# Two attention layers in fp32 on one core: the tensor engine in program order, steps of successive products alternating, eight score chunks in a row

## The chip, the cores and the metric

The kernel runs on one core of a Trainium2 chip. Of the engines of a core four matter here, each with its own queue of instructions: the tensor engine (PE, matrix products into PSUM), the vector engine (DVE), the scalar engine (ACT, activations and copies) and GpSimd (POOL); SyncE (SP) issues nearly all DMAs. The metric is the device time of one execution in microseconds.

## What is computed

Input x is 8 images of 512 channels by 32 x 32 = 1024 tokens, fp32. Two attention layers follow each other, each with a residual.

```python
def layer0(x):                                   # 8 heads of 64 channels
    h = group_norm(x, 32 groups)
    q, k, v = w_qkv @ h + b_qkv                  # 512 channels each
    weight = softmax(q^T k / 8)                  # per head, 1024 x 1024
    a = v @ weight^T
    return x + w_proj @ a + b_proj

def layer1(x):                                   # one head of 512 channels
    h = group_norm(x, 8 groups)
    q, k, v = q_w @ h + q_b, k_w @ h + k_b, v_w @ h + v_b
    attn = softmax(q^T k / sqrt(512))            # 1024 x 1024
    return x + p_w @ (v @ attn^T) + p_b
```

## The kernel before

An image is four chunks of 128 channels (KC = 4), two halves of 512 tokens (HT) or eight chunks of 128 tokens (NS). All matrix products are in fp32. The kernel folds layer 1's weights: w_m (from q_w and k_w) gives its scores as h^T (w_m h), and w_z (from v_w and p_w) gives its values already projected.

Per image b the text runs through these stages; those marked * work for image b + 1, since layer 0's q, k, v are made one image ahead, spilled to DRAM and fetched again:

1. layer 0's attention (`attention0`, L372);
2. v* (`by_token`, L296), the projection p (`by_channel`, L289, with `residual`, L621), q* and k* (`conv`);
3. g = w_m h (`conv`), layer 1's scores (`scores1`, L427, two products, one for each half of the first token axis), z = w_z h (`by_token`), the values (`values1`, L473), during which q, k, v of the next image are fetched (hooks, list `order`).

**The large products.** Each is one Strassen-Winograd product (`wino`, L202 to L239): seven products of half size, p = 1, 2, 6, 5, 7, 4, 3, called steps below. A step has two halves, i = 0 and 1, each of 128 output rows by 512 columns. Three PSUM tiles of two halves each, `psa`, `psb` and `psc`, collect them: steps 1 and 2 in a, steps 6, 7 and 4 in b, steps 5 and 3 in c. Within a step the text issues for each i the matmuls (`mm`) and then what reads that half of the tile: after step 1 ACT copies it to t1 (L223); after step 2 `done` makes a first quarter of the result; after 6 DVE makes u = psb + t1 (`upper`, L214); after 7 w, and a quarter from psc; after 4 and 3 the last two quarters. `done` is a copy, an exp with ACT, a bias with DVE (L327), a sum (L315, L450) or a residual (L624), according to the product. A step's matmuls per half are 2 with 512 columns (or 4 with 256), and 4 with 512 in `values1`; each fp32 matmul stands as two records in the trace. The operands of the seven products are sums of quarters, made on DVE (`left_sums` L140, `right_sums` L154), and put into the list `background`; after each step `run_background(back)` issues two or more entries of it, and `hooks` issues what is given for that step.

**Layer 0's attention.** A block is a pair of heads (hp) with a half of the tokens (tb): eight blocks per image. A score chunk is two matmuls of 64 rows, one for each head (L387), ACT's exp (L394) and DVE's running sum (L396, L398). The order of a block is four score chunks, four value chunks (L407, two matmuls of 64 columns), four score chunks, four value chunks. The row sums of a block (`reciprocals`, L340: matmuls with ones L352, reciprocal L354, minimum L355, POOL's sum L356, a DMA out and two back, L358 to L368, which spread r over partitions) are issued after the first four score chunks of the next block, and the product a = av x r (`scaled`, L420) after its second four. The list `extra` (entries for each half of a block) brings in the group norm and operand sums of the next image.

**Who sets the order.** The text gives the dependencies. Each engine's own order is decided by a scheduler with priorities, in before for PE too: it moves matmuls of neighbouring halves, steps, products and stages among each other. Pools: 33 slots of 4 KB per partition for images, factors and exps (`big`, NBIG), 3 PSUM tiles of two halves (`ps_sc`, for scores and for psa, psb, psc), 2 PSUM tiles of one half (`ps_acc`), 3 weight tiles (`wpool`), 1 slot for each of t, u, w and half (`upool`).

Of the kernel before, what the change touches and what calls it, by code (L numbers as in the profile page):

```python
# [9 lines left out]
F32 = mybir.dt.float32  # L10
# [7 lines left out]
NBIG = 33  # L18
# [10 lines left out]
def two_attention_blocks_kernel(  # L29
# [33 lines left out]

    def pcols(name):
        i = 4 * PARAMS.index(name)
        return par[:, i : i + 4]
# [14 lines left out]
    class GroupNorm:  # L81
# [18 lines left out]
        def group_mean(self, ps):  # L100
            mean, var = self.mv[:, :, 0], self.mv[:, :, 1]
            nc.tensor.matmul(ps, gm[:, self.layer, :], mean, start=True, stop=True)

            self.gmean = small.tile([P, KC], F32, tag="gmean", name=f"gmean_{self.uid}")
            nc.vector.tensor_copy(self.gmean, ps)
            d = small.tile([P, KC], F32, tag="d", name=f"d_{self.uid}")
            nc.vector.tensor_sub(d, mean, self.gmean)
            d2 = small.tile([P, KC], F32, tag="d2", name=f"d2_{self.uid}")
            nc.vector.tensor_mul(d2, d, d)
            self.dv = small.tile([P, KC], F32, tag="dv", name=f"dv_{self.uid}")  # L110
            nc.vector.tensor_add(self.dv, d2, var)

        def affine(self, ps):
            nc.tensor.matmul(ps, gm[:, self.layer, :], self.dv, start=True, stop=True)
# [39 lines left out]
    def right_sums(lo, hi, t124, sub):  # L154
# [4 lines left out]
        steps = []  # L159
        for j in range(n):  # L160
            steps.append(lambda j=j: sub(t1[j], b12[j], b11[j]))
            steps.append(lambda j=j: sub(t2[j], b22[j], t1[j]))  # L162
            steps.append(lambda j=j: sub(b12[j], b22[j], b12[j]))
            steps.append(lambda j=j: sub(t4[j], b21[j], t2[j]))
        return {1: b11, 2: b21, 3: b22, 4: t4, 5: t1, 6: t2, 7: b12}, steps

    def main_path(ctx):
# [34 lines left out]
        def wino(uid, mm, done, order=(1, 2, 6, 5, 7, 4, 3), hooks=(), back=2):  # L202
# [4 lines left out]
            ran = set()  # L207

            def u_tile(what, i):
                return upool.tile([P, HT], F32, tag=f"{what}{i}", name=f"{what}{i}_{uid}")  # L210
# [5 lines left out]
            for p in order:  # L216
                if bank[p] not in ps:
                    ps[bank[p]] = sc_tile(f"ps{bank[p]}_{uid}")
                for i in range(2):
                    mm(p, i, ps[bank[p]][:, i, :], bank[p] not in ran)  # L220
# [14 lines left out]
                ran.add(bank[p])  # L235
                run_background(back)
                if hooks:
                    for f in hooks.pop(0):
                        f()  # L239
# [49 lines left out]
        def by_channel(wf, hf, uid, done, **kw):  # L289
            def mm(p, i, ps, start):  # L290
                for k in range(2):
                    nc.tensor.matmul(ps, wf[p][:, k, ts(i, P)], hf[p][k], start=start and k == 0, stop=k == 1, skip_group_check=True)  # L292
# [3 lines left out]
        def by_token(wf, hf, name, **kw):  # L296
# [4 lines left out]
            def mm(p, i, ps, start):  # L301
                for jj in range(2):
                    for k in range(2):
                        nc.tensor.matmul(  # L304
# [35 lines left out]
        def reciprocals(total, uid, across):  # L340
# [6 lines left out]
            if across:  # L347
                sums = acc_tile(f"sums_{uid}")[:, : 2 * P].rearrange("p (a b) -> p a b", a=2)
            else:
                sums = sc_tile(f"sums_{uid}")[:, 0, : 2 * P].rearrange("p (a b) -> p a b", a=2)  # L350
            for i in range(4):
                nc.tensor.matmul(sums[ts(i, 32), :, :], ones[:, :32], total[:, :, ts(i, P)], start=True, stop=True)  # L352
# [19 lines left out]
        def attention0(b, q, k, v, extra):  # L372
            a = channel_tiles(f"a0_{b}")
            ending = []
            NB = 4
            for hp in range(KC):
                for tb in range(2):
                    uid = f"0_{b}_{hp}_{tb}"
                    total = pair_tile(f"sum_{uid}")
                    av = acc_tile(f"av_{uid}")  # L380
                    prev = None
                    for part in range(NS // NB):
                        es = []
                        for s in range(part * NB, (part + 1) * NB):
                            sc = sc_tile(f"sc_{uid}_{s}")
                            for j in range(2):
                                nc.tensor.matmul(  # L387
                                    sc[:, j, :],
                                    k[hp][j * 64 : (j + 1) * 64, ts(s, P)],
                                    q[hp][j * 64 : (j + 1) * 64, ts(tb, HT)],  # L390
                                    start=True, stop=True,
                                )
                            e = pair_tile(f"e_{uid}_{s}")
                            nc.scalar.activation(e, sc, AF.Exp, scale=(C // 8) ** -0.5)  # L394
                            if s == 1:
                                nc.vector.tensor_add(total, prev, e)  # L396
                            elif s > 1:
                                nc.vector.tensor_add(total, total, e)  # L398
                            prev = e
                            es.append(e)  # L400
                        if ending:
                            ending.pop(0)()
                        for f in extra.pop(0) if extra else ():
                            f()
                        for s in range(part * NB, (part + 1) * NB):
                            for j in range(2):
                                nc.tensor.matmul(  # L407
                                    av[j * 64 : (j + 1) * 64, :],
                                    v[s // 2][:, s % 2, hp * P + j * 64 : hp * P + (j + 1) * 64],
                                    es[s - part * NB][:, j, :],  # L410
                                    start=(s == 0), stop=(s == NS - 1),
                                )

                    r = {}

                    def sums(uid=uid, total=total, r=r):
                        r[0] = reciprocals(total, uid, False)

                    def scaled(hp=hp, tb=tb, av=av, r=r):
                        nc.vector.tensor_mul(a[hp][:, ts(tb, HT)], av, r[0])  # L420

                    ending += [sums, scaled]
            assert not extra
            return a, ending


        def scores1(b, gf, hf, uid):  # L427
# [5 lines left out]
            tiles = {}  # L433
            halves = lambda t: (t[:, :HT], t[:, HT:])
            ef = {p: [] for p in range(1, 8)}
            for j in range(2):

                def mm(p, i, ps, start):
                    for k in range(2):
                        nc.tensor.matmul(  # L440
# [29 lines left out]
                wino(f"sc_{uid}_{j}", mm, done)  # L470
            return e, total, ef

        def values1(b, zf, ef, r, xt, uid, hooks):  # L473
            def mm(p, i, ps, start):
                for k in range(4):
                    nc.tensor.matmul(  # L476
# [15 lines left out]
            wino(f"av_{uid}", mm, done, hooks=hooks)  # L492
# [9 lines left out]
        def natural(wt, nm):  # L502
            ts_ = [pair_tile(f"nat{nm}_{h}") for h in range(2)]
            t = [ts_[o // 2][:, o % 2, :] for o in range(KC)]
            for o in range(KC):
                pt = acc_tile(f"tr_w{nm}_{o}")
                for kc in range(KC):
                    nc.tensor.transpose(pt[:, ts(kc, P)], wt[kc][:, ts(o, P)], ident)
# [6 lines left out]
        def product(lhs, rhs, nm):  # L515
            ts_ = [pair_tile(f"prod{nm}_{h}") for h in range(2)]
            for ic in range(KC):
                ps = acc_tile(f"ps_w{nm}_{ic}")
                for kc in range(KC):
                    nc.tensor.matmul(ps, lhs[kc][:, ts(ic, P)], rhs[kc], start=(kc == 0), stop=(kc == KC - 1))  # L520
# [4 lines left out]
        def bias_product(dst, lhs, vec, add, nm):  # L525
            for oc in range(KC):
                ps = acc_tile(f"ps_b{nm}_{oc}")
                for kc in range(KC):
                    nc.tensor.matmul(
# [7 lines left out]
        def prologue():  # L537
# [7 lines left out]
            for c in range(KC):  # L545
                norm.stats(c, h0[c])
            product(wq, wk, "m")
# [8 lines left out]
            for n in "vqk":  # L556
                background.extend(first[n][1][:2])
                if n == "v":
                    background.extend(steps)
                background.extend(first[n][1][2:])  # L560
            v = by_token(weight_factors(first["v"][0]), hf, "v0_0", back=6)
# [7 lines left out]
            k = conv(weight_factors(first["k"][0]), hf, pcols("bk0"), "k0_0")  # L569
            norm1.group_mean(acc_tile("gmean_0_1")[:, :KC])  # L570
# [13 lines left out]
        for b in range(B):  # L584
# [12 lines left out]
            a, ending = attention0(b, q, k, v, extra)  # L597
# [4 lines left out]
            ends = [[ending[0]], [ending[1], lambda: background.extend(steps)]]  # L602
            spill = None
            if more:
# [6 lines left out]
                vn = by_token(weight("v"), hf0, f"v0_{b + 1}", hooks=ends)  # L611
                load_weight()
                store(2, vn)
# [18 lines left out]
            by_channel(weight("p"), af, f"p_{b}", residual)  # L632
            load_weight()
            run_background(len(background))
# [9 lines left out]
            if more:  # L644
                qn = conv(weight("q"), hf0, pcols("bq0"), f"q0_{b + 1}", hooks=[[mean], [], [affine], [normed]])
                load_weight()
                store(0, qn)
                background.extend(steps1)
                kn = conv(weight("k"), hf0, pcols("bk0"), f"k0_{b + 1}")
                load_weight()  # L650
                store(1, kn)
            else:
                mean()
# [3 lines left out]
            run_background(len(background))  # L657

            g = conv(weight("m"), hf1, ubias, f"g1_{b}")
            load_weight()  # L660
            stiles = [pair_tile(f"sg{i}_{b}") for i in (1, 2, 4)]
            halves = lambda t: (t[:, :HT], t[:, HT:])
            gf, steps = left_sums(
# [3 lines left out]
            background.extend(steps)  # L667
# [14 lines left out]
            z = by_token(weight("z"), hf1, f"z1_{b}", hooks=[[], [], [], [], [sums]], back=3)  # L682
            load_weight()
# [5 lines left out]
            zf, steps = left_sums(  # L689
# [3 lines left out]
            background.extend(steps)  # L693
# [3 lines left out]
            if more:  # L697
# [8 lines left out]
                for n, (i, c) in enumerate(order):  # L706
                    hooks[2 + n // 3].append(lambda i=i, c=c: fetch(i, c))
            values1(b, zf, ef, state["r"], xt, f"1_{b}", hooks)

# [11 lines left out]
        nc.tensor.matmul(ps[0:1, 0:1], both, ones[:, 0:1], start=True, stop=True)  # L721
        nc.vector.tensor_scalar(flag, ps[0:1, 0:1], -1.0, float(P), ALU.mult, ALU.add)

# [179 lines left out]
```

## Time and profile before

| | us |
|---|---|
| median of 3 runs | 3096.59 (3093.09 to 3098.21) |
| the profiled execution | 3092.8 |
| its span | 3090.9 |
| PE busy | 3042.8 (98%) |
| DVE busy | 1857.2 (60%) |
| ACT busy | 759.3 (25%) |
| POOL busy | 146.9 (5%) |
| image period (first score records at 527.0, 901.3, 1275.6, 1650.0) | 374.3 |

In a profile, a group of instructions is named by line, engine, operation and `out<-in`, with `x` for how many there are, then busy time, mean length of one, and the idle time of the engine just before them with what ended most of it. PEld is the load of the stationary operand. A matmul record's length reaches past the start of the next record, since matmuls are pipelined; the distance between starts tells how fast they stream. The largest groups off PE are the exps of layer 0 and the running sums:

```profile
L394 ACT ACTIVATE e<-sc 128x1024 f32<-128x1024 f32 x512 | 483.8, 1030 | 557.8 <-PE sc L387 550.9
L398 DVE TENSOR_TENSOR sum<-sum,e 128x1024 f32<-128x1024 f32 x384 | 466.3, 1214 | 74.7 <-ACT e L394 53.5
L354 DVE RECIPROCAL rc<-sums 128x256 f32<-128x256 f32 x72 | 125.9, 1749 | 14.9 <-issue 14.9
L420 DVE TENSOR_TENSOR a<-av,r 128x512 f32<-128x512 f32 x64 | 44.0, 688 | 33.6 <-DMA r<-rows 33.0
```

### The profile page before, as it was taken

The page shows a single profiled execution, that of the slowest core. Times are in us where ns is not written, and L with a number is a line of the kernel's source. Part 1 is how long each engine was busy: PE and PEld are TensorE (multiplying, and loading weights), DVE is VectorE, ACT ScalarE, POOL GpSimd, SP SyncE. Part 2 cuts the span into 40 slices and gives each one's busy share as a digit, 9 for nine tenths or more (in the row PEclk, how much of TensorE's full clock was granted, in tenths as well). Part 3 has the DMA queues.
Part 4 walks back from the last instruction along what each step waited for, and adds up shares of the span by engine and source line. Part 5 has one row for each costly group of instructions (what it writes and reads, how often), then busy time and mean ns, then how long its engine had stood idle before and what let it go on. Part 6 is the DMA issues. An engine that isn't in the chain of part 4 may idle for free. (4 is left out here: it accounts for less than half of the span.)

```text
span 3090.9 us, 26887 instructions
## 1 busy us (share of the span) xinstructions
PE 3042.8 (98%) x10322; PEld 1374.1 (44%) x10322; DVE 1857.2 (60%) x2445; ACT 759.3 (25%) x925; POOL 146.9 (5%) x119
## 2 busy tenths in 40 slices
PE   7999999999999999999999999999999999999898
PEld 5535444354543545335453354534445354443344
DVE  4376465864658646585366754567546764547754
ACT  1142111521124111351114411143111431105210
POOL 0000000000000000000000100000000000000000
PEclk9999999999999999999999999999999999999999
DMA  6412314023140332302332132411325023040101
GB/s 250 168 71 93 126 52 167 18 89 126 64 158 18 109 126 92 106 20 107 126 125 76 48 125 77 164 41 45 126 88 174 21 73 140 29 140 18 38 0 35
DMA packets 78295, 283.55 MB, mean 92 GB/s; under 512 B 9360, under 2 KB 16336, under 8 KB 71632
## 3 DMA queue, kind: packets, MB, share of 16 engines
q1 hardware_dynamic: 77744, 281.61, 25.8%
q8 instruction: 83, 1.36, 0.2%
q14 instruction: 52, 0.43, 0.0%
q10 hardware_dynamic: 416, 0.16, 0.0%
HBM read 207.51 MB, written 74.22 MB: 91 GB/s over the span
## 5 line engine op out<-in xcount | busy, mean ns | idle before, releaser
L394 ACT ACTIVATE e<-sc 128x1024 f32<-128x1024 f32 x512 | 483.8, 1030 | 557.8 <-PE sc L387 550.9
L398 DVE TENSOR_TENSOR sum<-sum,e 128x1024 f32<-128x1024 f32 x384 | 466.3, 1214 | 74.7 <-ACT e L394 53.5
L387 PE MATMUL sc<-q_again,k_again 64*128 64x512 f32 x1792 | 432.4, 603 | 0.0
L407 PE MATMUL av<-e,v_again 128*64 128x512 f32 x1792 | 409.2, 598 | 0.0
L387 PEld LDWEIGHTS sc<-q_again,k_again 64*128 64x128 f32 x1792 | 168.0, 186 | 260.7 <-issue 214.6
L407 PEld LDWEIGHTS av<-e,v_again 128*64 128x64 f32 x1792 | 118.6, 136 | 259.9 <-issue 224.8
L356 POOL TENSOR_TENSOR all_recs<-all_recs,rc 128x256 f32<-128x256 f32 x72 | 97.8, 1358 | 1604.6 <-DVE rc L354 1604.6
L440 PE MATMUL psa_sc<-g,h 128*128 128x512 f32 x256 | 125.4, 602 | 11.7 <-ACT t_sc L223 5.8
L354 DVE RECIPROCAL rc<-sums 128x256 f32<-128x256 f32 x72 | 125.9, 1749 | 14.9 <-issue 14.9
L396 DVE TENSOR_TENSOR sum<-e,e 128x1024 f32<-128x1024 f32 x64 | 78.3, 1224 | 91.1 <-ACT e L394 91.1
L451 ACT ACTIVATE e<-e 128x512 f32<-128x512 f32 x96 | 60.2, 630 | 261.3 <-DVE e L450 261.3
L476 PE MATMUL psa_av<-e,z 128*128 128x512 f32 x256 | 120.1, 601 | 0.0
L129 ACT ACTIVATE h<-h,b,s 128x1024 f32<-128x1024 f32 x30 | 37.1, 1240 | 192.0 <-DMA h<-in_x 158.9
L440 PEld LDWEIGHTS psa_sc<-g,h 128*128 128x128 f32 x256 | 46.7, 190 | 81.3 <-issue 47.8
L476 PEld LDWEIGHTS psa_av<-e,z 128*128 128x128 f32 x256 | 46.7, 190 | 53.2 <-issue 40.1
L292 PE MATMUL psa_g<-h,w_m 128*128 128x512 f32 x128 | 65.0, 622 | 4.0 <-ACT h L129 3.3
L214 DVE TENSOR_TENSOR u_sc<-psb_sc,t_sc 128x512 f32<-128x512 f32 x32 | 22.1, 691 | 77.0 <-PE psb_sc L440 77.0
L387 PE MATMUL sc<-q,k 64*128 64x512 f32 x256 | 65.3, 616 | 0.0
L214 DVE TENSOR_TENSOR w_sc<-psb_sc,t_sc 128x512 f32<-128x512 f32 x32 | 22.1, 691 | 71.8 <-PE psb_sc L440 71.8
L304 PE MATMUL psa_z<-w_z,h 128*128 128x256 f32 x256 | 64.6, 385 | 0.0
L420 DVE TENSOR_TENSOR a<-av,r 128x512 f32<-128x512 f32 x64 | 44.0, 688 | 33.6 <-DMA r<-rows 33.0
L440 PE MATMUL psc_sc<-sg,h 128*128 128x512 f32 x128 | 63.6, 599 | 0.6
(281 smaller groups left out, 4299.7 us busy)
## 6 DMA issues: line engine op xcount, KB each, us to landing
x<-in_x SPq DMA_DIRECT2D x36, 512.0 KB
h<-in_x SPq DMA_DIRECT2D x32, 512.0 KB
r<-rows SPq DMA_DIRECT2D x128, 128.0 KB
out<-x SPq DMA_DIRECT2D x64, 256.0 KB
w_p<-sums_p SPq DMA_DIRECT2D x8, 1792.0 KB
spill<-v SPq DMA_DIRECT2D x28, 512.0 KB
w_m<-sums_m SPq DMA_DIRECT2D x8, 1792.0 KB
spill<-q SPq DMA_DIRECT2D x28, 512.0 KB
```

What stands on the lines that cost most here:

```text
L292: nc.tensor.matmul(ps, wf[p][:, k, ts(i, P)], hf[p][k], start=start and k == 0, stop=k == 1, skip_group_check=True)
L304: nc.tensor.matmul(ps[:, ts(jj, C // 2)], hf[p][k][:, ts(2 * i + jj, P)], wf[p][:, k, :], start=start and (jj, k) == (0, 0), stop=(jj, k) ...
L354: nc.vector.reciprocal(rc, sums)
L356: nc.gpsimd.tensor_tensor(all_recs, all_recs, rc, ALU.add)
L387: nc.tensor.matmul(sc[:, j, :], k[hp][j * 64 : (j + 1) * 64, ts(s, P)], q[hp][j * 64 : (j + 1) * 64, ts(tb, HT)], start=True, stop=True,)
L394: nc.scalar.activation(e, sc, AF.Exp, scale=(C // 8) ** -0.5)
L396: nc.vector.tensor_add(total, prev, e)
L398: nc.vector.tensor_add(total, total, e)
L407: nc.tensor.matmul(av[j * 64 : (j + 1) * 64, :], v[s // 2][:, s % 2, hp * P + j * 64 : hp * P + (j + 1) * 64], es[s - part * NB][:, j, :], ...
L440: nc.tensor.matmul(ps, hf[p][k][:, ts(2 * j + i, P)], gf[p][k], start=start and k == 0, stop=k == 1, skip_group_check=True)
L451: nc.scalar.activation(dst, dst, AF.Exp, scale=scale)
L476: nc.tensor.matmul(ps, zf[p][k // 2][:, k % 2, ts(i, P)], ef[p][k], start=start and k == 0, stop=k == 3, skip_group_check=True)
```

## The change

- Every matmul and transpose goes through a local function that keeps it in program order on PE: PE now issues them as the text does. The other engines are still ordered by the scheduler.
- `wino` is cut into `step(p)`. A product issues its step 1, then `finish()`, the tail of the product before it (its steps 4 and 3, and the entries of `after`), then the four middle steps, (6, 2, 5, 7) or (2, 5, 6, 7), and leaves its own steps 4 and 3 as the next tail. The t tiles have two slots.
- What stood behind a product in the text (loads of weights, stores of the spill, operand sums of its result) moves into `after`; the hooks of q and values1 are regrouped; `values1` runs 4 background entries per step.
- `attention0` issues eight score chunks, then `scaled` of the block before, then eight value chunks, then its own row sums, in a `ps_acc` tile.
- `right_sums` lists its operations kind by kind; NBIG is 32; the prologue makes v's weight sums earlier.

```diff
+    def matmul(*args, **kw):
+        tc.keep_in_program_order(nc.tensor.matmul(*args, **kw))
...
-NBIG = 33
+NBIG = 32
...
-        def wino(uid, mm, done, order=(1, 2, 6, 5, 7, 4, 3), hooks=(), back=2):
+        tail = []
+
+        def finish():
+            while tail:
+                tail.pop(0)()
+
+        def wino(uid, mm, done, middle=(6, 2, 5, 7), hooks=(), after=(), back=2):
...
-            for p in order:
-                if bank[p] not in ps:
+            def step(p):
+                start = bank[p] not in ps
+                if start:
                     ps[bank[p]] = sc_tile(f"ps{bank[p]}_{uid}")
                 for i in range(2):
-                    mm(p, i, ps[bank[p]][:, i, :], bank[p] not in ran)
+                    mm(p, i, ps[bank[p]][:, i, :], start)
...
+            step(1)
+            finish()
+            for p in middle:
+                step(p)
+            tail.extend([lambda: step(4), lambda: step(3), *after])
...
-            if across:
-                sums = acc_tile(f"sums_{uid}")[:, : 2 * P].rearrange("p (a b) -> p a b", a=2)
-            else:
-                sums = sc_tile(f"sums_{uid}")[:, 0, : 2 * P].rearrange("p (a b) -> p a b", a=2)
+            sums = acc_tile(f"sums_{uid}")[:, : 2 * P].rearrange("p (a b) -> p a b", a=2)
...
+                    for s in range(NS):
+                        sc = sc_tile(f"sc_{uid}_{s}")
+                        for j in range(2):
+                            matmul(
+                                sc[:, j, :], k[hp][ts(j, 64), ts(s, P)], q[hp][ts(j, 64), ts(tb, HT)],
+                                start=True, stop=True,
+                            )
+                        e = pair_tile(f"e_{uid}_{s}")
+                        nc.scalar.activation(e, sc, AF.Exp, scale=(C // 8) ** -0.5)
...
+                    for f in extra.pop(0) if extra else ():
+                        f()
+                    if scaled:
+                        scaled()
                     av = acc_tile(f"av_{uid}")
...
+                    for s in range(NS):
+                        for j in range(2):
+                            matmul(
+                                av[ts(j, 64), :], v[s // 2][:, s % 2, hp * P + j * 64 : hp * P + (j + 1) * 64],
+                                es[s][:, j, :], start=(s == 0), stop=(s == NS - 1),
+                            )
+                    for f in extra.pop(0) if extra else ():
+                        f()
+                    r = reciprocals(total, uid, False)
...
-                vn = by_token(weight("v"), hf0, f"v0_{b + 1}", hooks=ends)
-                load_weight()
-                store(2, vn)
+                vn = by_token(
+                    weight("v"), hf0, f"v0_{b + 1}", hooks=ends, after=[load_weight, lambda: store(2, vn)]
+                )
...
-            wino(f"av_{uid}", mm, done, hooks=hooks)
+            wino(f"av_{uid}", mm, done, middle=(2, 5, 6, 7), hooks=hooks, back=4)
...
-                    hooks[2 + n // 3].append(lambda i=i, c=c: fetch(i, c))
+                    hooks[(2, 4, 5, 6)[n // 3]].append(lambda i=i, c=c: fetch(i, c))
             values1(b, zf, ef, state["r"], xt, f"1_{b}", hooks)
+            finish()
```

## The prediction

> **What bounds the kernel now.** I read the busy shares first, then the costliest groups for idle time with a releaser, then single stretches of the timeline in which the tensor engine (PE) changes its work.
>
> ```profile
> PE 3042.8 (98%) x10322; PEld 1374.1 (44%) x10322; DVE 1857.2 (60%) x2445; ACT 759.3 (25%) x925; POOL 146.9 (5%) x119
> PEclk9999999999999999999999999999999999999999
> L440 PE MATMUL psa_sc<-g,h 128*128 128x512 f32 x256 | 125.4, 602 | 11.7 <-ACT t_sc L223 5.8
> ```
>
> PE is busy for 98% of 3090.9 us, and at full clock in every slice. So a change can win only the remaining breaks, and any new break is paid in full. The last row shows the one kind of break that has a place: PE wants to write psa_sc and is held by ACT, which is still copying from it. This view is of one such place, with the columns start, length, engine and line, and in brackets the idle time before and what ended it:
>
> ```profile
> 400.91 1.98 PE L440 MATMUL psa_sc<-g,h 128*128 128x512 f32 x4 [0.72 <-ACT t_sc L223]
> ...
> 402.93 0.60 ACT L448 ACTIVATE e<-psa_sc 128x512 f32<-128x512 f32 x1 [2.07 <-PE psa_sc L440]
> 403.58 0.30 PEld L440 LDWEIGHTS psa_sc<-g,h 128*128 128x128 f32 x2 [1.51 <-ACT e L448]
> 403.58 1.98 PE L440 MATMUL psa_sc<-g,h 128*128 128x512 f32 x4 [0.69 <-ACT e L448]
> ...
> 405.40 1.88 PE L440 MATMUL psb_sc<-sg,t_h 128*128 128x512 f32 x4
> ...
> 407.12 1.02 PE L440 MATMUL psc_sc<-sg,t_h 128*128 128x512 f32 x2
> 407.39 0.69 DVE L214 TENSOR_TENSOR u_sc<-psb_sc,t_sc 128x512 f32<-128x512 f32 x1 [4.19 <-PE psb_sc L440]
> 408.13 0.30 PEld L440 LDWEIGHTS psb_sc<-sg,t_h 128*128 128x128 f32 x2 [0.82 <-DVE u_sc L214]
> 408.13 1.55 PE L440 MATMUL psb_sc<-sg,t_h 128*128 128x512 f32 x3
> ```
>
> A half step of a score product is four records of 512 columns. Streaming, they start 0.429 us apart (405.40 to 407.12 is four of them). The half from 400.91 should hand over at 402.62; the next half starts at 403.58. In between lies only the exp of the first half (402.93 to 403.53). The two halves are different parts of one tile, psa_sc, but the program's wait is for the tile. **Price of a direct wait behind ACT: 403.58 - 400.91 - 4 x 0.429 = 0.95 us.** At psb_sc the same wait, now behind DVE, is nearly hidden: the half ends its slots at 407.12, DVE reads it until 408.08, and two psc_sc records run meanwhile. Without them PE would stand from 407.12 to 408.13, and the first record after a wait takes 0.53 instead of 0.43: **1.01 + 0.10 = 1.11 us behind DVE.** So before is fast because its scheduler put something else between the halves.
>
> The attention blocks, and two score matmuls that were moved among layer 1's values:
>
> ```profile
> 505.89 1.12 PE L387 MATMUL sc<-q_again,k_again 64*128 64x512 f32 x2
> 506.94 3.70 PE L476 MATMUL psb_av<-e,z 128*128 128x512 f32 x8
> ```
>
> ```profile
> 548.36 3.70 PE L387 MATMUL sc<-q_again,k_again 64*128 64x512 f32 x16
> 551.99 3.65 PE L407 MATMUL av<-e,v_again 128*64 128x512 f32 x16
> 555.58 3.70 PE L387 MATMUL sc<-q_again,k_again 64*128 64x512 f32 x16
> 559.21 0.64 PE L352 MATMUL sums<-sum,ones 128*32 128x256 f32 x8
> ```
>
> Sixteen records of two heads run in pairs, eight slots of 0.429 = 3.43 us; 548.36 to 551.99 is 3.63 and 551.99 to 555.58 is 3.59. Entering the scores costs 0.20, entering the values 0.15.
>
> **The change, part by part.**
>
> *Program order in the large products.* In the built order of the changed kernel each matmul stands where the text issues it. Steps of successive products alternate, but within a step the half i=1 stands directly behind i=0. Every step except 5 has its first half read before the second is written, so it waits; and where two steps on one tile follow each other (6 then 7, or 7 then 4) it waits again. Counting in that order the PE instructions whose wait is on an ACT or DVE read of what the instruction just before it wrote gives 461: 129 behind ACT, 332 behind DVE, over 72 products. In the order of before I can tell 22 such waits; most of the others have one to three matmuls ahead of them. Cost: 129 x 0.95 + 332 x 1.11 = 123 + 369 = **+492**. Bounds: the shortest idle time in these rows (0.69) gives 318; the residual and bias reads take 0.75 instead of 0.69 (L624, L327), which on all 332 gives 512.
>
> *What those stages lose today.* Summed over every record, the time from start to start beyond the cadence is 194 us in the whole kernel, some 80 of it in the stages of large products (the rest: attention's changes of kind, the prologue, the last image's gaps). All of it is replaced: **-80**, bounds 0 and -94 (the latter by pricing each wait of before with the matmuls that stand between).
>
> *Split score pairs.* Before moves 34 single score matmuls of the next image among values1. Each runs alone for its two records (505.89 to 506.94 is 1.05 us), where half a pair is 0.43. Seventeen pairs lose 17 x 0.858 = 14.6, and their changes of kind, 34 x 0.35 = 12. After issues them in pairs: **-27**; if the pairs do not reunite, 0.
>
> *Eight chunks in a row.* One entry into the scores and one into the values less per block: 64 x (0.20 + 0.15) = **-22**. Exps on ACT start 0.917 us apart, chunks 0.858; with three score tiles chunk 7 needs exp 4 done at about 5.87 us of the block and starts at 6.11. Cover 0.24 us; if ACT were 0.1 us slower per exp, each block would lose about 0.2, 13 us in all.
>
> *Row sums at the end of the second product.* The sums (0.57 us, before after the first scores of the next block) now stand right after the eighth value chunk, at 14.1 us of the block, and the eighth running sum must be done: DVE needs 7 adds at 1.33 us after the second exp, about 12 us, if nothing is put in. In the built DVE order three blocks of an image have `scaled` (L420) among the adds, which waits for r; r lands 5.3 us after its reciprocal (562.95 to 568.27), so at 7.2 of the block. The adds then end at 14.55: 0.5 us lost in two blocks, and 2.0 in the one that also holds two factor operations of h. 3.0 per image: **+25**, bounds 0 (DVE catches up) and 64 x 2.0 = 128 if every block did this. What queues behind these sums on PE are the next block's scores, and on ACT its exps.
>
> *DVE's queue in the large products.* A wait behind DVE ends when DVE comes to it. In the built DVE order other work stands ahead of such reads: in the scores the sums of g and the subtractions (0.69 each: +1.55), four bn_stats of the image after next (4 x 0.67 = 2.6) and at z's step 6 1.0; 0.9 each in p and q. The scheduler in before lets PE go elsewhere meanwhile. 7.4 per image: **+60**, bounds 0 and 120 (each delay met twice, at both halves).
>
> *Slots, DMAs.* One big slot less, fetches regrouped over four steps, stores and weight loads issued one tail later. SP's queue carries them in the same order, and the fetched q, k land some 10 us before use (h's applies end at 517.9, paired scores start at 527). I cost them at 0; without that cover, one h apply (1.24 us) per chunk would show, 5 us per image, 40 in all.
>
> *The clock.* Before, the granted clock falls to half only after PE gaps of 3.5 us (at 37 and 2925 us); a gap of 3.0 us at 2919 did not do it, nor did halves in which PE stood for a third. After has one gap near 3.6 us per image (scores behind bn_stats). Half a window each is **+10**, bounds 0 and 24. A rule that speaks against the change: the Trainium skill, "TensorE: Matmul & The Clock Gate", section "A second HAM failure mode: psum-queue depth-cycling", says that small idle times of PE between groups of matmuls make its clock swing between half and full. The trace shows full clock through the waits at 400 to 409; by the rule part of the products would run at half speed, where by the trace none does.
>
> Sum: 3091 + 492 - 80 - 27 - 22 + 25 + 60 + 10 = **3549 us**. The profiled run took 3092.8, the median of the runs shown is 3096.6, so I add 3 and say **3552 us**.
>
> **The rivals.**
> - *DVE's queue becomes the bound of the products.* For it: 461 waits now expose every item of its queue, and DVE is already 60% busy. Against: ahead of most reads nothing stands. With twice the queue delays and reads of 0.75: 3552 + 60 + 20 + 14 (the clock's upper bound) = 3646, and up to 3720 with every block's sums late.
> - *The halves do not wait.* If hardware or program lets i=1 write its own half while i=0 is read, the waits fall away and so do today's breaks: 3552 - 492 - 60 - 10 = **2990**, faster. It decides once a direct wait costs under 104 / 461 = 0.23 us, 104 being what the change saves elsewhere (80 + 27 + 22 - 25). Against it: the rows at 403.58, where PE stood with nothing else to do.
> - *Only the shorter part shows.* If each wait costs what its idle column says (0.69 to 0.82) and DVE's queue nothing: 3552 - (492 - 350) - 60 = 3350.
> - *The clock swings.* If a quarter of the products' matmul work (64 of 56 slots and 8 of 112, at 0.429: 1922 us) runs at half clock: 3552 + 480 = 4030. Against: full clock in all slices of before, with 22 such waits, though never this dense.
>
> **How the numbers follow.** Forecast 0.74; DVE bound 0.1; shorter waits 0.08; clock 0.04; no waits 0.04, of which 0.01 ends within 0.2% (6 us, about what a measurement of this kernel can tell from no change). Faster 0.03, same 0.01, slower 0.96. The range goes from 3430 (each wait 0.2 shorter, 92, and half the queue delays, 30) to 3660 (DVE bound at twice its delays); about 0.2 is left out: the shorter waits, the clock, no waits and the upper end of the second case.
>
> **What would show it.** PE busy near 3000 us of a span near 3550, so 85%; about 460 idle times of PE ended by ACT L223, copies and exps, or by DVE u, w and final reads, 0.7 to 0.85 us each in the idle column; attention blocks of 14.65 us where before had 15.0; sums waiting for DVE's sum in three blocks per image; clock full. I am wrong if PE's large products show no idle time ended by the reads of their own tile, or if the clock line leaves 9.

## The result and the profile after

The changed kernel takes 3540.53 us (median of 4 runs, 3535.74 to 3544.32), against 3095.52 us for the kernel before: 1.1437 times as long, 95% interval 1.1417 to 1.1456. The forecast was 3552, in a range of 3430 to 3660. The profiled execution has a span of 3539.7 us at a mean granted clock of 0.988 (before: 3090.9 at 0.995).

These are lines of the page of the changed kernel. Every matmul now has line 66, since all go through the new function.

```profile
span 3539.7 us, 26844 instructions
...
PE 3090.2 (87%) x10322; PEld 1384.5 (39%) x10322; DVE 1853.0 (52%) x2445; ACT 755.2 (21%) x925; POOL 112.6 (3%) x119
...
PEclk9999999999999999999999999999999999999999
...
PE 51%; issue 17%; DVE 15%; ACT 2%; DMA 2%; POOL 1%; SPq 0%; DVEq 0%; ACTq 0%; POOLq 0%
...
L66 PE MATMUL psc_sc<-sg,h 128*128 128x512 f32 x128 | 72.6, 697 | 35.4 <-DVE e L451 35.4
```

PE has the same 10322 records and the other engines as many instructions as before, but PE is idle for 13% of a longer span, and the chain that ended last now has DVE in it for 15% and "issue" for 17% (before, it could be followed back over 6% of the span only, nearly all PE). The last row had 0.6 us of idle time before.

The timeline of layer 1's values shows where the time went (start, length, engine, line; in brackets the idle time before and what ended it):

```profile
572.86 3.60 PE L66 MATMUL psb_av<-t,sz 128*128 128x512 f32 x8
...
576.50 0.69 DVE L225 TENSOR_TENSOR u_av<-psb_av,t_av 128x512 f32<-128x512 f32 x1 [8.82 <-PE psb_av L66]
...
577.24 3.70 PE L66 MATMUL psb_av<-t,sz 128*128 128x512 f32 x8 [0.78 <-DVE u_av L225]
...
580.98 0.69 DVE L225 TENSOR_TENSOR u_av<-psb_av,t_av 128x512 f32<-128x512 f32 x1 [3.79 <-PE psb_av L66]
...
581.73 3.70 PE L66 MATMUL psb_av<-e,z 128*128 128x512 f32 x8 [0.78 <-DVE u_av L225]
...
585.46 0.69 DVE L225 TENSOR_TENSOR w_av<-psb_av,t_av 128x512 f32<-128x512 f32 x1 [3.79 <-PE psb_av L66]
...
586.21 3.70 PE L66 MATMUL psb_av<-e,z 128*128 128x512 f32 x8 [0.79 <-DVE w_av L225]
```

Eight records take 3.43 us of slots, and the halves follow each other at 4.38 to 4.49 us. Each time DVE reads the half just written for 0.69 us and PE does nothing. This is the forecast's direct wait, once per half.

To see the whole, I add for every PE record the time from the start of one to the start of the next beyond its cadence (0.429 us for 512 columns, 0.2146 for 256, a pair of heads counted once):

| us beyond cadence | before | after |
|---|---|---|
| large products, all | 101.9 | 570.1 |
| of it single breaks over 0.7 us (without the two at the group norm's last step) | 20.8 in 23 | 478.7 in 462 |
| attention: entries into scores and values | 54.3 | 26.4 |
| attention: row sums | 9.2 | 27.9 |
| group norm and prologue | 27.6 | 33.3 |
| slots of the work itself | 2885.9 | 2869.6 |

The sums over the rows without the second, which is part of the first, differ by +468.2 - 27.9 + 18.7 + 5.7 - 16.3 = 448.4; the spans differ by 448.8.

### The profile page after: what moved, and what is told of

Its sections match the earlier page's. It is cut to its first block, busy times and chain, and to the rows that moved or that the text cites. A ratio compares the mean times of both kernels' runs of the same rounds, so it can differ in the third digit from the quotient of the medians.

```text
span 3539.7 us, 26844 instructions
## 1 busy us (share of the span) xinstructions
PE 3090.2 (87%) x10322; PEld 1384.5 (39%) x10322; DVE 1853.0 (52%) x2445; ACT 755.2 (21%) x925; POOL 112.6 (3%) x119
## 4 chain that ended last, share of the span: by engine, by line
PE 51%; issue 17%; DVE 15%; ACT 2%; DMA 2%; POOL 1%; SPq 0%; DVEq 0%; ACTq 0%; POOLq 0%
PE sc L66 7%; PE av L66 6%; PE psb_av L66 5%; PE psb_sc L66 4%; DVE sum L405 4%; PE psa_av L66 3%; PE psc_av L66 3%; PE psa_sc L66 3%; PE psc_sc L66 3%; PE psb_g L66 3%; PE psb_k L66 2%; PE psb_z L66 2%; PE psa_g L66 2%; PE psc_g L66 2%; DMA r<-rows 2%
## 5 line engine op out<-in xcount | busy, mean ns | idle before, releaser
L401 ACT ACTIVATE e<-sc 128x1024 f32<-128x1024 f32 x512 | 476.4, 1054 | 541.6 <-PE sc L66 541.6
L66 PE MATMUL sc<-q_again,k_again 64*128 64x512 f32 x1792 | 399.7, 596 | 0.0
L66 PE MATMUL av<-e,v_again 128*64 128x512 f32 x1792 | 396.9, 596 | 0.0
L66 PEld LDWEIGHTS sc<-q_again,k_again 64*128 64x128 f32 x1792 | 167.3, 186 | 211.5 <-ACT e L401 101.9
L369 POOL TENSOR_TENSOR all_recs<-all_recs,rc 128x256 f32<-128x256 f32 x72 | 63.5, 882 | 1815.9 <-DVE rc L367 1815.9
L66 PE MATMUL psc_sc<-sg,h 128*128 128x512 f32 x128 | 72.6, 697 | 35.4 <-DVE e L451 35.4
L66 PE MATMUL psb_p<-t_a,w_p 128*128 128x512 f32 x128 | 64.9, 630 | 18.5 <-DVE x L631 6.7
L66 PE MATMUL psb_sc<-g,h 128*128 128x512 f32 x128 | 62.7, 612 | 19.4 <-DVE w_sc L225 12.5
L66 PE MATMUL psb_z<-w_z,t_h 128*128 128x256 f32 x256 | 67.4, 410 | 13.1 <-DVE u_z L225 6.8
L66 PE MATMUL psb_sc<-sg,t_h 128*128 128x512 f32 x128 | 65.4, 635 | 13.1 <-DVE u_sc L225 13.1
```

The source lines that it names most:

```text
L66: tc.keep_in_program_order(nc.tensor.matmul(*args, **kw))
L369: nc.gpsimd.tensor_tensor(all_recs, all_recs, rc, ALU.add)
```

## The experiments

Each was timed in turns with the kernel before on the same chip; ratios are to that.

**1. Both halves written before they are read.**

```diff
                 for i in range(2):
                     mm(p, i, ps[bank[p]][:, i, :], start)
+                for i in range(2):
                     if p == 1:
```

> The changed kernel, but in a step the matmuls of both halves are issued first and what reads the tile after them; PE stays in program order, the steps and all else as they are. If the loss is the wait of the second half for the reads of the first (theory), 421 of the 461 direct waits go, at 0.95 us each; left are the places where two steps on one tile follow each other (17 times 6 then 7, some 11 times 7 then 4), each now longer, about 1.7 us, since both halves are read after both are written. 3540 - 461 x 1.05 + 28 x 1.8 = about 3105, between 3070 and 3150. If the loss is strict order as such (weight loads that cannot run ahead, kinds of work that alternate more often) or DVE's queue, less than half of it goes: above 3330. If the clock is what costs, the granted clock rises from 0.988 and at most 30 us go.

Measured: 3062.33 us, ratio 0.9888 (0.9872 to 0.9905), clock 0.992. The same stretch of the timeline, PE alone:

```profile
491.31 7.03 PE L66 MATMUL psb_av<-t,sz 128*128 128x512 f32 x16
499.79 7.13 PE L66 MATMUL psb_av<-e,z 128*128 128x512 f32 x16 [1.45 <-DVE u_av L225]
508.30 7.13 PE L66 MATMUL psb_av<-t,z 128*128 128x512 f32 x16 [1.38 <-DVE w_av L225]
515.27 5.31 PE L66 MATMUL psc_av<-e,sz 128*128 128x512 f32 x12
```

Sixteen records run without a break; breaks stand here only where step 7 follows 6, and 4 follows 7, on psb. None between 0.7 and 1.15 us is left in the products of the whole trace; 88 of their 570 us beyond cadence are left (38.5 of them in the values). So one line of order, with program order, steps and attention untouched, takes back more than the whole loss. Strict order on PE is no burden as such: this is 1.1% faster than the kernel before. A scheduler that orders PE freely in this text, with both halves written first, was not run.

**2. The change without program order, and 3. program order without the change.**

```diff
-        tc.keep_in_program_order(nc.tensor.matmul(*args, **kw))
+        nc.tensor.matmul(*args, **kw)
```

> The changed kernel without program order: PE's order is the scheduler's again, all else as changed. Theory: the scheduler puts other matmuls between the halves (18 direct waits behind DVE and 10 behind ACT in its built order, against 332 and 129), so the products cost what they cost before, and attention keeps its gain of some 20 us: 3050 to 3095. If the new order of steps or the tails cost by themselves, it stays above 3200.

Measured: 3103.77 us, ratio 1.002 (1.001 to 1.003), 9 us above the upper end expected. The waits are gone as the theory says: 34 breaks over 0.7 us are left in the products, 32.4 us in all. But of the gain in attention most is gone too. From the start of each record to the next, scores, values and row sums together take 982.9 us here, 990.0 in the kernel before and 964.2 in the changed kernel. And the products take 13.6 us more than in the kernel before: 15 of the 34 breaks, 0.95 each, are waits behind w in the values, where the kernel before has one.

> The kernel before with program order on PE and nothing else. Its text has the halves one behind the other too, and the steps of one product in a row: 548 direct waits in the built order (180 behind ACT, 368 behind DVE). Theory: 3096 + 180 x 0.95 + 368 x 1.05 - 80 (its own breaks) - 27 (split pairs) + 40 (DVE's queue) = about 3585, between 3520 and 3660: slower than the changed kernel, so that alternating steps helped a little and program order alone makes the loss. If the loss needs the other edits, it stays near 3100.

(The same function as in the changed kernel, around every matmul and transpose of the kernel before.) Measured: 3616.08 us, ratio 1.1679 (1.166 to 1.1699); expected 3585, 3520 to 3660. Two lines of its page:

```profile
span 3613.4 us, 26948 instructions
...
PE 3121.4 (86%) x10322; PEld 1357.8 (38%) x10322; DVE 1877.7 (52%) x2445; ACT 763.4 (21%) x925; POOL 146.9 (4%) x119
```

Program order alone makes the loss: the trace has 548 breaks over 0.7 us in the products, as many as were counted ahead. The loss is larger than in the changed kernel; by the traces 58 of the 74 us between the two lie in the products.

**4. The old attention in the changed kernel, and 5. the new attention in the kernel before.** Only `attention0`, its row sums' tile and its ending are exchanged.

```diff
-            a, scaled = attention0(b, q, k, v, extra)
+            a, ending = attention0(b, q, k, v, extra)
```

> The changed kernel with the attention of before: four score chunks, four value chunks, row sums after the first scores of the next block; the rest as changed. Theory: eight in a row saves 22 and the row sums at the end lose about 20, so the two attentions cost nearly the same here (the 27 us of split pairs come from program order and stay): 3540 within 10. If eight in a row is worth its 22 and the sums at the end cost nothing, it is 3562; if the sums are the larger, below 3530.

Measured: 3535.56 us (3534.01 to 3543.23) beside 3540.53: the same within their spread, as the theory has it. Beyond cadence, its entries cost 48.6 us against 26.4 in the changed kernel, and its row sums 9.3 against 27.9: eight chunks in a row win 22.2 and the row sums at the end give 18.6 back, so the new attention is some 4 us the faster. The products of this run are 8.6 us shorter than the changed kernel's, since fewer stretches of half clock fall into them (see the last section).

> The kernel before with the new attention alone (eight chunks in a row, row sums at the end), PE's order left to the scheduler. The forecast's terms give 3096 - 22 + 25 = 3099. The changed kernel without program order came out at 3104 and had 164 score matmuls that stood alone instead of 68 in before; if the new attention brings these, this run is at 3100 to 3110 with as many of them; if the new order of steps does, it is at 3099 or below with about 70.

Measured: 3094.43 us, ratio 0.9989 (0.9979 to 0.9999), as the second case has it. The count in the expectation was a wrong reading, though: 164 is the number of score records in run 2 (two to a matmul) without a partner that starts within 25 ns, and here there are 168. Most of these do run in twos, with the partner up to 312 ns behind. Layer 1's values, the first scores of a block after them, and last the same place in the kernel before:

```profile
511.10 1.12 PE L380 MATMUL sc<-q_again,k_again 64*128 64x512 f32 x2
512.16 3.70 PE L462 MATMUL psb_av<-e,z 128*128 128x512 f32 x8
...
532.22 6.27 PE L380 MATMUL sc<-q_again,k_again 64*128 64x512 f32 x26
538.42 1.94 PE L398 MATMUL av<-e,v_again 128*64 128x512 f32 x8
```

```profile
527.00 2.84 PE L387 MATMUL sc<-q_again,k_again 64*128 64x512 f32 x10
529.77 3.65 PE L407 MATMUL av<-e,v_again 128*64 128x512 f32 x16
```

The 26 records take 6.20 us to the first value, which is 14 slots of 0.429 and the entry of 0.20, and the 10 in the kernel before take 2.77, 6 slots and the entry. Thirteen and five slots would do if every record shared its slot, so in each case one matmul runs alone, beside the three that stand among the values. Counted so (a partner within 300 ns), 68 records run alone in the kernel before, in run 2 and here. A free scheduler moves the same few score matmuls out under either attention, and each holds PE for two slots instead of sharing them. That loss, priced in the prediction, stays in runs 2 and 5 and goes with program order.

**6. One tile for each half, in one place.**

```diff
+                    if two and p == 5:
+                        ps["c"] = [acc_tile(f"psc{i}_{uid}") for i in range(2)]
```

> The changed kernel, but in layer 1's two score products psc is two tiles of one half each (from the pool of the row sums), so that step 3's second half need not wait for the read of its first. Order and work are as changed; 16 direct waits of 461 go (316 behind DVE instead of 332). Theory: the wait is the program's, by tile, and the chip can write one half while the other is read: 14 of these waits were 2.58 us long in the changed kernel's trace, since DVE had sums or statistics ahead, and two about 1; with the slower first records and the clock drops that follow the long ones 16 x 0.1 and 14 x 0.7 more: 3540 - 38 - 2 - 10 = 3490, between 3480 and 3505. If the chip itself held the write until the read is over, the time would stay at 3540.

Measured: 3497.01 us (3496.45 to 3499.68), 43.5 less than the changed kernel. The changed kernel first, then this one, at step 3 of the first score product:

```profile
481.15 1.88 PE L66 MATMUL psc_sc<-sg,h 128*128 128x512 f32 x4
...
482.20 0.68 DVE L451 TENSOR_TENSOR e<-psb_sc,t_sc 128x512 f32<-128x512 f32 x1
...
483.58 1.23 DVE L458 TENSOR_TENSOR sum<-sum,e 128x1024 f32<-128x1024 f32 x1 [0.69 <-ACT e L452]
484.72 0.68 DVE L451 TENSOR_TENSOR e<-psc_sc,u_sc 128x512 f32<-128x512 f32 x1
...
485.46 1.62 PE L66 MATMUL psc_sc<-sg,h 128*128 128x512 f32 x2 [2.43 <-DVE e L451]
```

```profile
480.05 3.60 PE L66 MATMUL psc_sc<-sg,h 128*128 128x512 f32 x8
...
482.48 1.22 DVE L462 TENSOR_TENSOR sum<-sum,e 128x1024 f32<-128x1024 f32 x1 [0.69 <-ACT e L456]
...
483.48 1.88 PE L66 MATMUL psb_sc<-sg,t_h 128*128 128x512 f32 x4
...
483.62 1.28 DVE L455 TENSOR_TENSOR e<-psc_sc,u_sc 128x512 f32<-128x512 f32 x2
```

In the changed kernel the first half could be read at about 483, but DVE first waits for an exp and adds a running sum for 1.23 us; PE stands for 2.43 us behind it. With two tiles the eight records run through, and DVE reads both halves later. So the wait belongs to the tile. At two of the sixteen places DVE is early enough to read the first half while PE writes the second; this is one:

```profile
3050.95 3.60 PE L66 MATMUL psc_sc<-sg,h 128*128 128x512 f32 x8
...
3052.87 0.69 DVE L455 TENSOR_TENSOR e<-psc_sc,u_sc 128x512 f32<-128x512 f32 x1
```

The second half's four records start at 3052.67 and stream on at 0.43 us while DVE reads, so the chip does not hold the write here. The gain is made up otherwise than the theory has it. The 16 waits, 38.1 us, are gone, but part of what DVE had ahead is met at later waits (the one behind u on psb grows from 0.98 to 1.55 us in the mean), so that all breaks together fall by 26 us; the rest is mainly the half clock that followed the long breaks.

**7. What alternating the steps is worth.** Program order and both halves first, in the kernel before, whose steps of one product stand in a row.

```diff
+        tc.keep_in_program_order(nc.tensor.matmul(*args, **kw))
...
                     mm(p, i, ps[bank[p]][:, i, :], bank[p] not in ran)
+                for i in range(2):
                     if p == 1:
```

> The kernel before with program order on PE and both halves of a step written before they are read; its steps stay 1, 2, 6, 5, 7, 4, 3 of one product in a row, its attention is the old one. What is left are waits where two steps on one tile follow each other: 1 then 2 and 7 then 4, 52 behind ACT and 64 behind DVE stand directly behind each other in the built order. Theory: two reads now end such a wait, about 1.4 us behind ACT and 1.6 behind DVE: 73 + 102 = 175, against some 50 in the changed kernel with both halves first (3062): about 3187, between 3150 and 3230. That would be what alternating the steps is worth. If alternating is worth nothing beyond the halves, it is at 3062.

Measured: 3217.94 us, ratio 1.0394 (1.0378 to 1.041), in the expected range. The trace has 117 breaks over 0.7 us in the products, 172.8 us (116 and 175 were expected), against 38 and 60.4 in run 1. The two runs differ by 156 us, and their spans by 155; 131 of that lie in the products, 17 in the attention with its row sums, the rest in the prologue and the group norm. So alternating steps, with the regrouped operand sums that belong to it, is worth some 130 us once the halves don't wait; with waiting halves (run 3 and the changed kernel) it was worth 58.

**8 to 10. Towards a faster version**, each on top of the one before.

```diff
-            wino(f"av_{uid}", mm, done, middle=(2, 5, 6, 7), hooks=hooks, back=4)
+            wino(f"av_{uid}", mm, done, middle=(2, 6, 5, 7), hooks=hooks, back=4)
```

> The version with both halves written before they are read, and values1's middle steps as 2, 6, 5, 7 instead of 2, 5, 6, 7, so that step 5 lies between the two steps on psb. Theory: the eight waits of 1.61 us at 6 then 7 go: 3062 - 13 = 3049. If step 6's operand (a sum on DVE, issued after step 2) is late, up to 1.5 us come back per image: 3061.

Measured: 3048.49 us, ratio 0.9836 (0.982 to 0.9853). As expected: the eight breaks are gone from the trace, since step 5 now covers the reads of step 6.

```diff
-                    if scaled:
-                        scaled()
                     av = acc_tile(f"av_{uid}")
...
+                    if scaled:
+                        scaled()
                     r = reciprocals(total, uid, False)
```

> As the one before, and in attention the product a = av x r of the last block is issued after the value chunks, behind the running sums. Theory: the row sums' waits for DVE (0.3 to 1.6 us in three blocks per image, 15 us above 0.5 and 23 in all) shrink: 3049 - 15 = 3034. If the scheduler puts the product where it was, or the value tile is then freed too late for the next row sums, no change or slower.

Measured: 3049.36 us, ratio 0.9841 (0.9825 to 0.9858): no change. DVE's order is the scheduler's, and the product stayed among the running sums.

```diff
-                            nc.vector.tensor_add(total, total, e)
+                            tc.keep_in_program_order(nc.vector.tensor_add(total, total, e))
...
-                        nc.vector.tensor_mul(a[hp][:, ts(tb, HT)], av, r)
+                        tc.keep_in_program_order(nc.vector.tensor_mul(a[hp][:, ts(tb, HT)], av, r))
...
+                    for _ in range(2):
+                        for f in extra.pop(0) if extra else ():
+                            f()
                     r = reciprocals(total, uid, False)
...
-                    extra[8 + i].append(f)
+                    extra[8 + i].append(lambda f=f: tc.keep_in_program_order(f()))
```

> The version with both halves first and 2, 6, 5, 7 in values1 (3048), and in attention DVE in program order for the running sums, the product a = av x r and the operand sums of h, all of the latter two behind the running sums of their block. Theory: the row sums' waits go (23 us of 27 in the trace of that version), and a later reciprocal costs nothing, since the first running sum has 0.8 us to spare: 3048 - 20 = 3028. If the running sums themselves are late behind the reciprocal and the operand sums, the waits of one or two blocks per image stay: 3040. If it is above 3048, holding DVE's order costs more than it saves.

Measured: 3030.55 us (3028.32 to 3031.22), ratio 0.9782 (0.9769 to 0.9796), near the 3028 expected. First a block of the changed kernel whose row sums wait:

```profile
675.57 5.32 PE L66 MATMUL av<-e,v_again 128*64 128x512 f32 x24
...
679.91 1.29 DVE L166 TENSOR_TENSOR t_h<-h 128x512 f32<-128x512 f32 x2
681.12 1.22 DVE L405 TENSOR_TENSOR sum<-sum,e 128x1024 f32<-128x1024 f32 x1
...
682.39 0.64 PE L66 MATMUL sums<-sum,ones 128*32 128x256 f32 x8 [1.50 <-DVE sum L405]
```

and then a block of this version:

```profile
568.23 7.88 DVE L406 TENSOR_TENSOR sum<-sum,e 128x1024 f32<-128x1024 f32 x6
...
570.76 7.09 PE L66 MATMUL av<-e,v_again 128*64 128x512 f32 x32
...
576.02 0.68 DVE L423 TENSOR_TENSOR a<-av,r 128x512 f32<-128x512 f32 x1
...
577.78 0.64 PE L66 MATMUL sums<-sum,ones 128*32 128x256 f32 x8
...
578.35 7.14 PE L66 MATMUL sc<-q_again,k_again 64*128 64x512 f32 x32
```

In the first, two operand sums of h stand ahead of the last running sum and PE waits 1.50 us for it. In the second, six running sums go in a row, the product behind them is over at 576.70, and PE goes from values to row sums to scores without idle time. No block's row sums wait for DVE any more. This version is 2.2% faster than the kernel before, with all of its work.

## Why the prediction was right

The mechanism is the one forecast, and the sum came out 12 us above the time. That it is so near has some luck in it: DVE's queue was put 23 us too high and the clock some 15 too low. By its own terms, with what the trace after shows (beyond cadence):

- **Direct waits, +492 for 461.** 462 breaks over 0.7 us are there. 421 of them lie between 0.7 and 1.15 and sum to 402.3, 0.96 each; with the slow first record behind a wait, some 0.1, that is within the priced 0.95 to 1.11, and all 462 at that price are some 490. Runs 1 and 6 remove them by the text's order and by the tile, and the time follows; run 3 makes them without the rest of the change. This cause is shown.
- **Before's own losses, -80.** The products lost 101.9, of which 7.1 are two breaks at the last image's and the prologue's group norm, and those stay. In the changed kernel less than 20 of the products' 570.1 are neither a break over 0.7, nor a slow first record, nor half clock, so over 80 were replaced.
- **DVE's queue, +60.** Too large. Over a plain 0.96 the 41 breaks above 1.15 us hold 37 us (and the items listed add to 7.0 per image, not 7.4). The place was right in part: 14 of them, of 2.6 us, are at psc of the scores. In the second product they stand behind the statistics of a later image, as forecast, but in the first behind a running sum, which the forecast did not name; z's step 6 shows no delay (1.01), its step 3 does (1.34).
- **Split pairs -27 and entries -22.** The slots of the work fell by 16.3, the entries by 27.9: 44 of 49. Run 4 gives the entries of eight chunks in a row alone as 22.2.
- **Row sums, +25.** 18.7, in the three blocks per image that were named.
- **Clock, +10.** Too small, and its reading of the kernel before was wrong. There the clock fell at 37.4, before PE's break began (37.8 to 41.1), and at 2925.1, 0.9 us into the second of two breaks, so neither fall shows that a break of 3.5 us is needed. In the changed kernel eleven stretches of half clock, 3.4 us each, follow breaks of 2.6 us and cost 1.7 each, 19 us; longer ones in the prologue and at the last image cost some 6 more than in the kernel before. Run 6, without these breaks, has 0.993 instead of 0.988. The rule weighed in the prediction (the Trainium skill, "TensorE: Matmul & The Clock Gate", section "A second HAM failure mode: psum-queue depth-cycling") did not bite in general: the clock line stays at 9 throughout, with a break of about 0.95 us after nearly every other half.
- **PE busy near 3000, 85%.** It shows 3090.2 and 87%, because a record's modelled end reaches past its slot and part of each break counts as busy. The starts, not the busy time, show the breaks.
- **Slots and DMAs, 0.** Held: past the prologue no idle time of PE is ended by a DMA.

What the forecast did not see is how close the change was to a gain. With a step's reads behind both of its halves, and nothing else altered, it is 1.1% faster than the kernel before (run 1).

## What to carry to other kernels

Before an engine is put in program order, go through the text for places where it writes a tile that another engine has just been told to read: each costs the whole read plus both handovers, here 0.95 to 1.05 us, and a scheduler that filled it before is no longer there. Write all parts of a tile first and read them afterwards, and put a step on another tile between. Where an engine stays with the scheduler, moving a line in the text may move nothing (run 9): look at the order that was built.

## What the runs showed of the hardware

A break of 2.6 us beyond cadence, in which PE is idle for 2.4 us, can be enough to lower the clock, but is not always. Two stretches of the changed kernel with the same break and the same shorter one before it, with the granted clock after the busy times of the five engines:

```profile
481.00:490.00 9.00, 6.57 (x12) 2.58 (x11) 6.24 (x8) 1.72 (x3) 0.56 (x1) 0.81 0.00 1
912.60:921.60 9.00, 5.78 (x14) 2.11 (x12) 6.99 (x10) 1.89 (x3) 0.52 (x1) 1.00 0.00 0
```

In the first, PE is idle from 483.0 to 485.5 and the clock is at half from 486.0 to 489.4; in the second, PE is idle from 914.6 to 917.0 and the clock stays full. Of the 14 such breaks in the scores of the changed kernel 11 were followed by half clock, beginning 2.7 to 3.8 us after the start of the break; in run 4, with the same breaks, 4 of 14. In run 1 a break of 2.4 us of idle time at 1330.9, with no other over 0.6 us in the 9 us before it, was followed by half clock too. So neither the length of a break nor a shorter one before it decides alone; what does was not tried.
